# Keys and the second layer's first product as seven products of quarters, in a two-layer graph kernel on one core

## The chip, the cores and the metric

The kernel runs on one core of a Trainium2 chip. The metric is the device time of one launch in microseconds, and less is better. The engines are named as the profile names them: PE (TensorE, matrix products), DVE (VectorE), ACT (ScalarE), POOL (GpSimd), and SP (SyncE, whose queue issues most of the loads). Each engine takes its instructions in the order in which the kernel issued them, and waits at each for what it needs from the others.

## The reference, cut to what matters

There are 16 graphs of 1024 nodes and 256 channels, which share one adjacency matrix. Layer 0 is attention whose queries come from a product with a weighted adjacency, and layer 1 is a graph convolution with two dense products and batch norms over all graphs.

```
# layer 0, per graph; h = relu(layernorm(x))
Wg  = adj * A_s(mean of h)                       # 1024 x 1024
q   = relu((h^T @ Wg) * para)                    # "queries"
k,v = split(h @ kv_w)                            # "keys", "values"
x   = x + softmax(q k^T) v                       # 4 heads
# layer 1; h = relu(layernorm(x))
agg = (D^-1/2 (adj + I) D^-1/2) @ h              # "aggregate"
y1  = agg @ W1^T + b1                            # 256 -> 512, "hidden"
out = batchnorm(relu(batchnorm(y1)) @ W2^T + b2) # needs all graphs
x   = x + out
```

## The kernel before, in words

All numbers are float32. The first part of the kernel, `layers`, handles the 16 graphs one after the other; the second part, `second`, runs the last product and the batch norms once all graphs have gone through. The change is in the first part, whose order is written out by hand.

**Attention sets the beat.** `attention` (L1092) goes through 16 steps for each graph. A step issues two tiles of scores (`scores`, L923: PE products `sc`, then the exponential on ACT into `p`), then the two additions of `p` to the running sums (`Unit.add`, L956, on DVE: `acc`), then the product of the previous step's `p` with the values (`Unit.values`, L967, PE: `o`). There are two score tiles in PSUM and four `p` tiles in SBUF.

**The rest is background.** While graph b is in attention, `background(b)` (L835) does the other work in small pieces: graph b+1's keys, values and queries, and graph b-1's second norm, aggregate and hidden product. Each piece yields a cost (1.71 for two products), and `attention` takes pieces at the end of each step until the sum of their costs reaches what is due (`total`, L1108). A side generator in `weave` (L148) is advanced once with each piece of the main one. An action given to `soon` (L128) is issued after the next piece. So the order of the instructions on every engine follows from these costs.

**Pieces that the change touches.**
- `product` (L167) is one product of 128 x 128 by 128 x 512, in two halves of 64 rows. `bank` (L164) gives it one of the three PSUM tiles of `ps_mm` (L118), in turn; a tile comes round again at the third next call, and its first product then waits until the reader of the old contents is done.
- `keys_values` (L649): four keys banks of two products each (L657), copied by ACT (L660), then four values banks (L669), copied by ACT (L677).
- `weigh` (L454) makes the weighted adjacency: 17 slots, in turn two ACT operations `Abs` (L485), one `Tanh` (L493), and with every second slot one DVE operation (L472).
- `queries` (L514) makes its product as seven products of quarters, each four inner products long; `take` (L548) and `finish` (L534) are DVE work. Its four `para` loads (L528) go round two buffers, so each waits on SP until the user of the buffer before is done.
- `aggregate` (L682) is also seven products of quarters. Its 14 loads `aht` (L693) go on SP's queue, five ahead, into the buffers of the weights `w`. Four DVE operations scale its result by the roots of the degrees (`scale`, L705).
- `hidden` (L757): eight banks of two products, each read by ACT with the bias (L773), written out by a DMA on POOL's queue (L774), with statistics on DVE (L777).
- `normed` (L790) writes x away (`keep`), normalises, and loads the graph after the next two (L796). `load_x` (L173) goes round three buffers.
- `graph` (L244), once, in graph 0's background: POOL combines quarters of the adjacency and writes them out as `aht_d`. `degrees` (L225), once, computes the degrees. `load_later` (L290), once, loads W1 and broadcasts the roots.
- `differences` (L428) sends the column sums of a graph out and broadcasts them back into `cbc`, which the `Abs` operations read.
- `prepare` (L812) issues a graph's transposition by way of DRAM (`squares`, `gathered`) and its first weight slots along with the hidden product.

Seven products of quarters means the Winograd form of Strassen's method: for a product of two 2 x 2 arrangements of blocks, seven block products in place of eight, with sums of blocks before and after.

Of the kernel before, what the change touches and what calls it, by code (L numbers as in the profile page):

```python
# [17 lines left out]
P = 128  # L18
# [5 lines left out]
def gnn_two_layers_kernel(  # L24
# [34 lines left out]
    vec = const.tile([P, 18], F32, name="vec")  # L59
    nc.sync.dma_start(out=vec, in_=vecs)  # L60
    b1, g1, be1 = (vec[:, i * HC : (i + 1) * HC] for i in range(3))
    b2, g2, be2 = (vec[:, 3 * HC + i * CC : 3 * HC + (i + 1) * CC] for i in range(3))
# [34 lines left out]
    def layers(shifted):  # L97
# [13 lines left out]
        py = st.enter_context(tc.tile_pool(name=f"py_{kind}", bufs=4))  # L111
# [7 lines left out]

        xs, hs, hts, ats, qs, ks, vs = {}, {}, {}, {}, {}, {}, {}  # L120
        invs = {}
        csums, cbcs, weighted, weighers = {}, {}, {}, {}
# [50 lines left out]
        def load_x(b):  # L173
            xs[b] = p3.tile([P, NT, C], F32, tag="x", name=f"x_{b}")
            parts = 4 if b == 0 else 2
            for part in range(parts):
                t = slice(part * NT // parts, (part + 1) * NT // parts)
                nc.sync.dma_start(
                    out=xs[b][:, t], in_=x[b].rearrange("(t p) c -> p t c", p=P)[:, t]
                )  # L180
# [44 lines left out]
        def degrees():  # L225
# [16 lines left out]
            rsqrt(dinv, deg, 1.0, tmp_deg)  # L242

        def graph():  # L244
# [21 lines left out]
            for u in range(2 * HT):  # L266
# [3 lines left out]
                for n in range(2):  # L270
                    if part == t * P // HB:
                        blk = a[:, n, n, t * P % HB : t * P % HB + P]
                        nc.gpsimd.tensor_add(blk, blk, ident)
                two = py.tile([P, 2, HB], F32, tag="y", name=f"two_{u}")
# [14 lines left out]

        def load_later():  # L290
            later["w1"] = big.tile([P, CC, H1], F32, tag="w1", name="w1")
            nc.sync.dma_start(out=later["w1"], in_=w1_t.rearrange("(k p) j -> p k j", p=P))
            later["dbc"] = const.tile([P, N], F32, tag="dbc", name=f"dbc_{kind}")
            nc.sync.dma_start(out=dinv_d.rearrange("(t p) -> p t", p=P), in_=dinv)
            nc.sync.dma_start(
                out=later["dbc"], in_=dinv_d.rearrange("(o n) -> o n", o=1).to_broadcast([P, N])
            )

        class Norm:
# [3 lines left out]
            def __init__(self, b, first):  # L303
                tag = "a" if first else "b"
                self.src = xs[b]
# [343 lines left out]
        def keys_values(b):  # L649
            ht = hts[b]  # L650
            ks[b] = [p4.tile([P, N], F32, tag="k", name=f"k_{b}_{k}") for k in range(CC)]
            for g in range(NH):
                for j in range(CC):
# [7 lines left out]
                    yield 1.71  # L661

            vs[b] = [p4.tile([P, NT, P], F32, tag="v", name=f"v_{b}_{k}") for k in range(CC)]
# [18 lines left out]
        def aggregate(b):  # L682
# [3 lines left out]
            order = (0, 2, 5, 1, 4, 6, 3)  # L686
# [18 lines left out]
            def scale(c, g):  # L705
                nc.vector.tensor_mul(c, c, later["dbc"][:, g * FB : (g + 1) * FB])

# [4 lines left out]
            def second(m):  # L712
                add(c11, m, c12)
                sub(a12, a12, a11)
                soon(lambda: scale(c11, 0))

            def fifth(m):
                add(c22, m, c21)
                add(c12, m, c12)
                soon(lambda: scale(c22, 1))  # L720

            def sixth(m):
                add(c21, m, c21)
                soon(lambda: scale(c21, 0))

            def seventh(m):
                add(c12, m, c12)
                scale(c12, 1)

            for i, (left, after) in enumerate(  # L730
# [5 lines left out]
                    (None, fifth),  # L736
                    (a22, sixth),
                    (a12, seventh),
# [4 lines left out]
                for th in range(NP // 2):  # L743
# [9 lines left out]
                    elif i == 0:  # L753
                        combine("b", b, nc.vector)
                    yield 1.71

        def hidden(b):  # L757

# [31 lines left out]
        def normed(b):  # L790
# [4 lines left out]
            if b + 3 < B:  # L795
                load_x(b + 3)  # L796
# [15 lines left out]
        def prepare(b, products):  # L812
# [4 lines left out]
            if b == 2:  # L817
                for k in range(CC):
                    yield from weave(islice(products, 3), (0, islice(w, AHEAD // 2)))
                    yield TOP  # L820
                    transposed(b, (k,))
                    yield 1.0
                yield from products
                return
            squares(b)
            yield from weave(islice(products, 3), (0, islice(w, AHEAD // 2)))
            gathered(b, 0)
            yield from weave(islice(products, 1), (0, islice(w, 1)))
            gathered(b, 1)
            yield from weave(islice(products, 2), (0, islice(w, AHEAD // 2 - 1)))  # L830
# [4 lines left out]
        def background(b):  # L835

            if b == 0:
# [6 lines left out]
                yield from weave(  # L844
# [719 lines left out]
```

## Time and profile before

| What | us |
|---|---|
| Median of the 3 runs (2488.99 to 2489.55) | 2489.24 |
| The profiled execution | 2488.76 |
| Its span, first to last instruction | 2487.0 |
| PE clock granted, mean | 0.993 |
| Start of graph 1, 2, 3 in attention | 166.9, 304.1, 440.1 |
| ACT L660, copies of keys, 64, each | 0.579 |
| ACT L773, hidden product with bias, 128, each | 0.683 |
| DVE L706, scaling of the aggregate, 64, each | 0.674 |
| DVE L965, addition to the sums, 384, each | 1.227 |
| DVE L734, addition from PSUM, 16, each | 0.685 |

The profile is of one execution. A group of its instructions has a line of the kernel, an engine, the output and the inputs by their names in the program, the count, the busy time and the mean of one, and then the time for which the engine had been idle, with what ended it. In a timeline the columns are start and duration in us, engine, line, operation and operands, and how many instructions were merged into the row.

### The profile page before, as it was taken

How to read it: one execution, taken by the hardware profiler on the slowest of the kernel's cores; microseconds unless marked ns; L12 is line 12 of the kernel's file. 1: busy time of each engine (PE TensorE's matmuls, PEld its weight loads, DVE VectorE, ACT ScalarE, POOL GpSimd, SP SyncE). 2: the span in 40 equal slices, each digit the busy share in tenths (PEclk: the TensorE clock that was granted, in tenths of full speed). 3: DMA queues.
4: the chain of work that ended last, by engine and by line, in shares of the span. 5: the costliest groups of instructions: out<-in, count | busy, mean ns of one | idle time of the engine just before them, and what ended most of it. 6: DMA issues, size and time to landing. Idle time of an engine off the chain costs nothing. (4 is left out here: it accounts for less than half of the span.)

```text
span 2487.0 us, 35569 instructions
## 1 busy us (share of the span) xinstructions
PE 2435.7 (98%) x13403; PEld 841.2 (34%) x13403; DVE 1882.0 (76%) x2920; ACT 1401.7 (56%) x1927; POOL 429.2 (17%) x527
## 2 busy tenths in 40 slices
PE   9999999999999999999999999999999999999995
PEld 4333333333333333333333333333333332334444
DVE  5668787877778787878787787868787877767775
ACT  7775564647473746656474747465564634345544
POOL 1640101010101001011101010110101001036652
PEclk9999999999999999999999999999999999999997
DMA  4754535354545545362645445543536344355559
GB/s 150 238 173 172 170 114 199 101 199 129 197 145 178 164 159 169 116 206 84 215 126 182 145 174 169 178 153 132 191 94 210 116 140 162 132 214 220 189 199 374
DMA packets 187909, 421.42 MB, mean 169 GB/s; under 512 B 21832, under 2 KB 81744, under 8 KB 181968
## 3 DMA queue, kind: packets, MB, share of 16 engines
q1 hardware_dynamic: 158560, 311.56, 37.9%
q0 software_dynamic: 29168, 107.50, 11.6%
q8 instruction: 108, 1.77, 0.3%
q14 instruction: 73, 0.60, 0.1%
HBM read 315.63 MB, written 103.35 MB: 168 GB/s over the span
## 5 line engine op out<-in xcount | busy, mean ns | idle before, releaser
L941 ACT ACTIVATE p<-sc 128x1024 f32<-128x1024 f32 x512 | 494.9, 1019 | 617.6 <-PE sc L933 617.2
L965 DVE TENSOR_TENSOR acc<-acc,p 128x1024 f32<-128x1024 f32 x384 | 471.3, 1227 | 165.1 <-ACT p L941 143.8
L933 PE MATMUL sc<-q,k 64*64 64x512 f32 x4096 | 498.8, 602 | 6.2 <-ACT p L941 6.2
L976 PE MATMUL o<-p,v 128*64 128x512 f32 x2048 | 494.5, 604 | 0.3 <-DVE os L990 0.3
L171 PE MATMUL pg<-w,h_a 128*64 128x512 f32 x1600 | 359.8, 592 | 0.8 <-DVE w L472 0.8
L171 PE MATMUL pa<-aht,h_b 128*64 128x512 f32 x1536 | 346.0, 592 | 1.1 <-ACT h_b L342 1.0
L485 ACT ACTIVATE w<-cbc,csum 128x512 f32<-128x512 f32 x256 | 285.8, 1168 | 0.0
L933 PEld LDWEIGHTS sc<-q,k 64*64 64x64 f32 x4096 | 131.0, 132 | 347.9 <-issue 286.5
L472 DVE SCALAR_TENSOR_TENSOR w<-w,adj 128x1024 f32<-128x1024 f32 x128 | 156.9, 1225 | 95.0 <-ACT w L493 91.1
L171 PE MATMUL py<-at,w 128*64 128x512 f32 x1024 | 228.4, 592 | 0.2 <-ACT y L773 0.2
L976 PEld LDWEIGHTS o<-p,v 128*64 128x64 f32 x2048 | 124.4, 136 | 298.3 <-issue 260.3
L994 POOL DMA_DIRECT2D out_d<-os x58 | 34.2, 590 | 1070.8 <-DVE os L990 1037.5
L171 PEld LDWEIGHTS pg<-w,h_a 128*64 128x64 f32 x1600 | 114.8, 137 | 229.2 <-issue 218.8
L171 PEld LDWEIGHTS pa<-aht,h_b 128*64 128x64 f32 x1536 | 109.9, 137 | 215.3 <-issue 202.0
L773 ACT ACTIVATE y<-py,vec 128x512 f32<-128x512 f32 x128 | 87.4, 683 | 115.4 <-PE py L171 91.8
L493 ACT ACTIVATE w<-w 128x1024 f32<-128x1024 f32 x128 | 135.1, 1055 | 1.7
L774 POOL DMA_DIRECT2D y_d<-y x128 | 69.7, 545 | 371.8 <-ACT y L773 362.6
L548 DVE TENSOR_TENSOR w<-w,w 128x1024 f32<-128x1024 f32 x112 | 132.7, 1214 | 1.5
L171 PEld LDWEIGHTS py<-at,w 128*64 128x64 f32 x1024 | 74.0, 137 | 145.5 <-issue 131.5
L171 PE MATMUL pv<-kvw_f,ht 128*64 128x256 f32 x1024 | 116.1, 379 | 0.0
L171 PE MATMUL pk<-ht,kvw_f 128*64 128x512 f32 x512 | 115.2, 592 | 0.2 <-ACT ht L404 0.2
L342 ACT ACTIVATE h_b<-x,lnsm_b 128x256 f32<-128x256 f32 x128 | 69.9, 599 | 65.9 <-DVE lnsm_b L331 65.9
(169 smaller groups left out, 2665.4 us busy)
## 6 DMA issues: line engine op xcount, KB each, us to landing
aht<-aht_d SPq DMA_DIRECT2D x224, 512.0 KB, 6.4
adj<-in_adj_dram SPq DMA_DIRECT2D x128, 512.0 KB, 4.8
y_d<-y POOLq DMA_DIRECT2D x128, 256.0 KB, 3.0
yin_f<-y_d SPq DMA_DIRECT2D x32, 1024.0 KB, 6.4
para<-in_para_dram SPq DMA_DIRECT2D x64, 256.0 KB, 3.6
x_d<-x POOLq DMA_DIRECT2D x16, 1024.0 KB, 5.2
xo_f<-x_d SPq DMA_DIRECT2D x32, 512.0 KB, 8.2
out_dram<-xo_f POOLq DMA_DIRECT2D x32, 512.0 KB, 10.8
```

What stands on the lines that cost most here:

```text
L171: nc.tensor.matmul(dst[r], left[:, r], right, start=start, stop=stop)
L342: nc.scalar.activation(self.h[:, t, :], self.src[:, t, :], AF.Relu, bias=self.sm[:, 1, t : t + 1], scale=self.sm[:, 0, t : t + 1], accum_o ...
L472: nc.vector.scalar_tensor_tensor(w, w, 1.0, a, op0=ALU.add, op1=ALU.mult)
L485: nc.scalar.activation(w[:, t, :].rearrange("p (t q) -> p t q", q=P), cbc[:, q * NT // NH : (q + 1) * NT // NH], AF.Abs, bias=csum[:, th * ...
L493: nc.scalar.activation(made[i], made[i], AF.Tanh, scale=-0.5 / C)
L548: nc.vector.tensor_sub(block(i)[part], block(x)[part], block(y)[part])
L773: nc.scalar.activation(y, made, AF.Identity, bias=b1[:, j : j + 1])
L774: nc.gpsimd.dma_start(out=y1_d[i][:, j, :], in_=y)
L933: nc.tensor.matmul(sc[part, e, :], ks[b][k][r, m * P + c * HW : m * P + (c + 1) * HW], qs[b][k][r, f * FB : (f + 1) * FB], start=True, sto ...
L941: nc.scalar.activation(pr, sc, AF.Exp)
L965: nc.vector.tensor_add(self.acc, self.acc, pr)
L976: nc.tensor.matmul(self.o[r, :], vs[b][k][:, m, r], pr[:, e, :], start=(m == 0), stop=(m == NT - 1),)
```

## The change

- **Keys** of graphs 3 to 15 (`keys_of`, behind `values_of`): seven products of quarters, one product to a bank, on blocks of the transposed h. ACT copies two of the seven banks, DVE adds the other five into the result. POOL makes two sums of blocks before (`key_steps`), two in between, and two sums of results.
- **Hidden product** of graphs 0 to 13: twice seven products, one product to a bank, in an order written out. ACT reads four of the 14 banks, DVE ten. POOL adds four times. The blocks' sums are made at the end of the aggregate (`steps_of`, three subtractions on DVE) and at the start of the hidden product (one). Graphs 14 and 15 keep the old form (`plain_hidden`).
- **Weights**: eleven slots of `weigh` go one to a piece with the values and keys, the others one to a piece with the queries (before: four, then two to a piece). In `background(b)`, from b = 2 on, all values and keys stand ahead of the queries; before, the values stood behind them.
- **x** is loaded twice, into one buffer for each use: `xn` for the first norm, at the start of `background`, and `xr` for the residual, at the end of `normed`. The first output of a graph is added one step later than before (`wait` 6 for 5).
- **The scaling by the roots of the degrees** moves from DVE in each aggregate to POOL in `graph`, once; the roots are broadcast at the end of `degrees`, ahead of `differences(2)`, and `graph` runs from the end of graph 0's background into graph 1's.
- The sums of blocks of the weights are made once, on POOL (`combined` in `load_later`). The tiles `y` are six for four. The last two products of the aggregate change places. The costs that pace the background follow.

```diff
         def keys_values(b):
+            if b > 2:
+                yield from values_of(b)
+                yield from keys_of(b)
+                return
...
+        def keys_of(b):
...
+            t1, t2 = steps.pop(b)
+            nc.gpsimd.tensor_sub(b12, b22, b12)
+            add = nc.vector.tensor_add
+
+            def second(m):
+                add(c11, m, c12)
+                nc.gpsimd.tensor_sub(b21, b21, t2)
+
+            def fifth(m):
+                add(c21, m, c12)
+                nc.gpsimd.tensor_add(c12, c12, c22)
+                nc.gpsimd.tensor_add(c22, c22, c21)
+
+            for i, (left, right, after) in enumerate(
+                (
+                    (a11, b11, lambda m: nc.scalar.copy(c12, m)),
+                    (a12, b21, second),
+                    (s1, t1, lambda m: nc.scalar.copy(c22, m)),
+                    (s2, t2, lambda m: add(c12, m, c12)),
+                    (s3, b12, fifth),
+                    (s4, b22, lambda m: add(c12, m, c12)),
+                    (a22, b21, lambda m: add(c21, m, c21)),
+                )
+            ):
+                made = bank(f"pk_{b}_{i}")
+                product(made, left, right, True, True)
+                after(made)
+                yield 0.86
...
         def hidden(b):
+
+            if b >= B - 2:
+                yield from plain_hidden(b)
+                return
...
+            def m1(c):
+                part = one("1", a11, c, b11)
+                nc.scalar.activation(
+                    new("11", c), part, AF.Identity, bias=b1[:, c : c + 1]
+                )
+
+            def m2(c):
+                y = made["11"]
+                add(y, one("2", a12, c, b21), y)
+                put(y, 0, c)
+
+            def m3(c):
+                y = made["12"]
+                add(y, one("3", s4, c, b22), y)
+                put(y, 1, c)
+
+            def m4(c):
+                y = made["21"]
+                add(y, one("4", a22, c, t4), made["sum"])
+                put(y, 0, 2 + c)
+
+            def m5(c):
+                nc.scalar.copy(new("22", c), one("5", s1, c, t1))
+                if c == 1:
+                    both(c)
+
+            def both(c):
+                nc.gpsimd.tensor_add(new("12", c), made["21"], made["22"])
+
+            def m6(c):
+                y = new("21", c)
+                add(y, one("6", s2, c, t2), made["11"])
+                if c == 0:
+                    both(c)
+
+            def m7(c):
+                part, y = one("7", s3, c, t3), made["22"]
+                nc.vector.scalar_tensor_tensor(
+                    new("sum", c), part, b1_step[:, c : c + 1], made["21"], op0=ALU.add, op1=ALU.add
+                )
+                nc.gpsimd.tensor_add(y, y, made["sum"])
+                put(y, 1, 2 + c)
+
+            for c, order in ((0, (m1, m5, m6, m2, m3, m7, m4)), (1, (m1, m6, m2, m5, m7, m3, m4))):
+                for each in order:
+                    each(c)
+                    yield 0.86
...
             yield from Norm(b, False).all()
-            if b + 3 < B:
-                load_x(b + 3)
+            load_x(b + 1)
...
             rsqrt(dinv, deg, 1.0, tmp_deg)
+            dbc = big.tile([P, 4, H1 // 2], F32, tag="w1s", name="dbc")
+            dbc = later["dbc"] = dbc.rearrange("p a b -> p (a b)")
+            nc.sync.dma_start(out=dinv_d.rearrange("(t p) -> p t", p=P), in_=dinv)
+            nc.sync.dma_start(
+                out=dbc, in_=dinv_d.rearrange("(o n) -> o n", o=1).to_broadcast([P, N])
+            )
...
+                dinvs = later["dbc"].rearrange("p (m c) -> p m c", m=NH)[:, :, cols]
+                for n in range(2):
+                    nc.gpsimd.tensor_mul(a[:, n], a[:, n], dinvs)
+                yield 0.0
...
             gather = aggregate(b - 1)
             if b + 1 < B:
                 w, products, norm = weighers[b + 1], keys_values(b + 1), normed(b - 1)
-                yield from weave(islice(products, 4), (0, islice(w, 4)))
+                build = later.pop("graph", iter(()))
                 if b == 1:
...
                     load_later()
-                yield from weave(queries(b + 1), (0, double(w)), (9, islice(norm, 5)))
+                else:
+                    yield from weave(products, (0, islice(w, 11)))
+                    yield from weave(queries(b + 1), (0, w), (6, norm))
                 yield next(gather)
                 yield from weave(products, (0, norm))
```

## The prediction

> **What bounds the kernel now.** I read the page first, for the busy shares, then who made PE wait, then one graph in the middle (847.9 to 983.9 us) by stretches, then the timelines of PE, ACT, DVE and SP through that graph.
>
> ```profile
> PE 2435.7 (98%) x13403; PEld 841.2 (34%) x13403; DVE 1882.0 (76%) x2920; ACT 1401.7 (56%) x1927; POOL 429.2 (17%) x527
> ```
>
> Busy share alone does not settle it, so the next view is PE's waits (total us, times, longest):
>
> ```profile
> PE sc L933 <- ACT p L941: 6.2, 5, 2.5
> ...
> PE pa L171 <- ACT h_b L342: 1.0, 1, 1.0
> ...
> PE py L171 <- ACT y L773: 0.2, 1, 0.2
> ```
>
> The whole list, 14 rows, comes to 21 us. One graph of the steady middle, in four stretches summed:
>
> ```profile
> sum 136.00, PE 136.00 PEld 43.97 DVE 107.24 ACT 78.40 POOL 14.16; mean PE 34.00 PEld 10.99 DVE 26.81 ACT 19.60 POOL 3.54
> ```
>
> PE is busy for 136.00 of 136.00 us. Every graph from 2 to 13 starts 135.96 us after the one before. So each microsecond of PE taken away is a gain, and each one in which PE must wait is a loss. Nothing else counts here.
>
> The price of a product comes from PE's timeline (start, us; the first row of each step is sc):
>
> ```profile
> 883.65 1.95 PE L933 MATMUL sc<-q,k 64*64 64x512 f32 x16
> 885.52 1.94 PE L976 MATMUL o<-p,v 128*64 128x512 f32 x8
> 887.29 3.60 PE L171 MATMUL pg<-w,h_a 128*64 128x512 f32 x16
> 890.83 1.95 PE L933 MATMUL sc<-q,k 64*64 64x512 f32 x16
> 892.70 1.94 PE L976 MATMUL o<-p,v 128*64 128x512 f32 x8
> 894.47 5.32 PE L171 MATMUL pg<-w,h_a 128*64 128x512 f32 x24
> 899.72 1.95 PE L933 MATMUL sc<-q,k 64*64 64x512 f32 x16
> ```
>
> A step with two parts of background lasts 7.18 us (883.65 to 890.83), one with three 8.89: a part of two products costs 1.71, one product 0.857, scores and values 3.7.
>
> **The gain.** Keys of graphs 3 to 15 need 7 products for 8: 13 fewer. The second layer's first product of graphs 0 to 13 needs 14 for 16: 28 fewer. 41 x 0.857 = 35.1 us. The profiled execution took 2488.76 (span 2487.0; median of the runs 2489.24), so with nothing else changed 2453.6.
>
> **What evacuates the products.** Before, a bank of these two stages held two products (1.71 us) and ACT emptied it. Now each product has its own bank (still three in ps_mm), so a bank must be emptied within two further products, 1.71 us, and mostly by DVE. Per graph DVE gets 10 adds for the second layer, 4 subtractions for its steps and 5 adds for the keys, and loses 4 scalings: 15 x 0.69 (rows of 128x512) = 10.4 us, 107.2 to 117.6 of 133.4 us. That fits on average. But in each step the two acc additions stand ahead of the background's work in DVE's order, and they wait for the step's exponentials on ACT. That order sets three stalls. Below, t is counted from the start of step 0 of a graph, with distances between starts in the timelines.
>
> **Keys (step 2).** The changed order puts the four value products and all seven key products into steps 0 to 2, with one weight slot on each. ACT has no idle time from the first value product (t = 5.6) on. Up to the exponentials of step 2 it has four pairs of value copies (0.52 each), four pairs of L485 (2.25), three L493 (0.95), two key copies (0.48) and the exponentials of step 1 (1.84): 2.1 + 9.0 + 2.8 + 1.0 + 1.8 = 16.7. So those of step 2 start at t = 22.4, 5.4 into the step. The old kernel shows the same lateness (step 2 began at 865.74, its exponentials at 871.54):
>
> ```profile
> 866.27 1.06 ACT L493 ACTIVATE w<-w 128x1024 f32<-128x1024 f32 x1
> ...
> 868.18 2.37 ACT L485 ACTIVATE w<-cbc,csum 128x512 f32<-128x512 f32 x2
> 870.58 1.06 ACT L493 ACTIVATE w<-w 128x1024 f32<-128x1024 f32 x1
> 871.54 1.92 ACT L941 ACTIVATE p<-sc 128x1024 f32<-128x1024 f32 x2
> ```
>
> ```profile
> 872.58 2.56 DVE L965 TENSOR_TENSOR acc<-acc,p 128x1024 f32<-128x1024 f32 x2 [2.28 <-ACT p L941]
> ```
>
> The acc pair then takes 23.4 to 25.8, and the add that empties the fourth key product ends at 26.4. The seventh takes the same bank and is due at 16.9 + 3.7 + 3 x 0.857 = 23.2. PE stands for **3.2 us**. The old kernel bore this because ACT emptied its key banks in ACT's own order and a query product fills a bank for 3.4 us. Lower end: exponentials 1 us earlier, 2.2. Upper: POOL's two additions on c12 and c22 collide with DVE's weight product (below), 4.0. 13 graphs: 42 us (29 to 52).
>
> **Second layer's first product (steps 13 to 15).** t' from step 13. DVE: acc to 4.4, one subtraction, two squares 2.3 (to 7.35), two adds (8.6), transpose and sum (9.95); step 14: acc after the exponentials to 12.6, m3's add 13.2, a weight product 14.35, statistics 14.95, m7's add 15.65. The fifth product after m3 (m6 of the second half) needs m7's bank, and would start at 14.3: it waits **1.4 us**. The walk of step 15 finds no further wait. Lower 0.5, upper 3 if DVE enters step 13 late. 13 graphs: 19 us (6 to 39).
>
> **Loads (step 8).** SP takes its DMAs in order. Before, the order was para, os, five aht, then x:
>
> ```profile
> 868.87 37.97 SPq L528 DMA_DIRECT2D para<-in_para_dram  x3
> 906.93 1.80 SPq L1000 DMA_DIRECT2D os<-out_d  x4
> 908.85 2.49 SPq L693 DMA_DIRECT2D aht<-aht_d  x5
> 916.77 0.94 SPq L178 DMA_DIRECT2D x<-in_x_dram  x2
> ```
>
> The last para waited for DVE's product with an earlier para until 906.84; aht went at 908.85, 6.9 us ahead of pa (915.73), and lands in 4.3 to 10.2. In the changed order the queries start three key products later, pa follows them at once (the four value products that lay between are gone to the front), and the reload of x, which waits for the last h_b, stands ahead of aht. Walking DVE on from the key stall (steps 5 and 6 hold 13.2 and 8.6 us of rows against 8.9 and 8.9 of PE), the para product ends 1.3 us into step 8. Then para, two x (0.94 us of issue) and aht: aht leaves about 3 us into step 8 behind 1.25 MB. At 0.41 MB/us (DMA packets of the trace between 912 and 916, summed), with 2 us to the first bytes, it lands at 8 us; pa is due at 3.8. Stall 4.2 by the walk, 0.1 if DVE were not late, 5.5 if it is later still. I take **3.5**, nearer the walk since DVE was 5 us late at this place already (897.58 for exponentials ready by 893). 13 graphs: 46 us (1 to 72). The reload itself (1 MB a graph more) is due only two steps later and is covered.
>
> The rest of the change costs nothing that I can find: the tail after graph 15 is the same code, the output of each graph's first unit is added two steps later and nothing waits for it but the next norm, and the DVE scalings that go were off PE's path.
>
> **Graphs 0 and 1, once.** The roots of the degrees are now written to DRAM and broadcast back ahead of the column sums of graph 2, on the same queue. What SP waited for then (120 to 260 us):
>
> ```profile
> SPq L295 <- DMA dinv_d<-deg: 10.4, 1, 10.4
> ...
> SPq L450 <- DMA csum_d<-csum: 3.9, 1, 3.9
> ```
>
> The degrees are ready at 139.7, the root at 142; 10.4 us for the write, then 3.9 for the sums' write and 5.8 for their broadcast (its landing before): 163. ACT's first weight of graph 2 now stands at step 12 (about 146 us into the span; 153 before) and blocks the exponentials behind it. Two score buffers cover one step: some 13 us later. POOL then scales and combines the adjacency with 16 more operations of 128x512; with 12 us a piece for eight pieces it ends near 250, about when graph 0's aht is wanted: 5 more. 18 us (5 to 30).
>
> **POOL beside DVE.** An operation of 128x512 on POOL does not occur before; 128x256 takes 0.73 and 128x1024 2.36, so 1.2 to 1.5, ten a graph. What one does to DVE is seen once at the end (start, us):
>
> ```profile
> 2227.67 2.67 DVE L1382 TENSOR_TENSOR y_f<-y_f,y_f 128x512 f32<-128x512 f32 x1
> ```
>
> ```profile
> 2227.45 2.35 POOL L1327 TENSOR_TENSOR t_f<-yin_f,yin_f 128x1024 f32<-128x1024 f32 x1
> ```
>
> An addition of 0.68 with both inputs in SBUF took 2.67, until POOL was through. On the 13 acc additions that met a POOL operation the mean is 1.48 for 1.22, so ten cost 2.6 us a graph, which is inside the upper ends. The Trainium skill (SBUF — State Buffer, Who interferes with whom) has it as an exclusive lock held for the whole instruction, the other fully blocked; if all ten met the start of one, DVE would lose some 12 us a graph and have 129 of 133 us filled. That would speak against the change even on average.
>
> **Sum.** 2488.8 - 35.1 + 42 + 19 + 46 + 18 = 2578.7. I forecast **2578**.
>
> **Rivals.**
> Loads hidden: DVE catches up while PE stands at the keys, para is free in step 7 and aht is in time. Without that term 2533. For it: the x load of before rode behind aht with no wait. Against: order on SP.
> Evacuation in time, faster: 2454, or 2472 with the loss in graphs 0 and 1. For it: PE waits for nothing now, DVE has 24% left. It decides only if the exponentials of step 2 start 3.2 us earlier (t = 19.2), so that the fourth key bank is empty in time, and the aht loads leave in step 7. Against it: the ACT sum above has no idle time in it to give back.
> The port of DVE and POOL makes DVE the bound in steps 0 to 3 and 13 to 15, so that the 2.6 us a graph reach PE: 13 x 2.6 = 34 more, 2612.
> That the products are not fewer is excluded: the built order of PE has three fewer in each graph from 2 to 13.
>
> **Numbers.** All three stalls, 2550 to 2600: 0.50. Loads hidden, 2495 to 2550: 0.25. Port, 2600 to 2650: 0.12. In time, 2454 to 2484: 0.10. Between, within 0.2% of before (5 us, about what a measurement of this kernel can tell from no change): 0.03. So slower 0.87, same 0.03, faster 0.10. The lower ends of the terms sum to 2495, the upper ones to 2647; the range 2495 to 2625 leaves out the faster case (0.10), no change (0.03) and the upper half of the port's (0.06).
>
> **What would show it.** In the new profile: PE waiting for DVE k at the keys' product, 13 times near 3 us; for DVE y at py, near 1.4; for DMA aht at pa, 13 times some 3 to 4; a gap of ACT near 146 to 163 and PE sc waiting for ACT p there. Graphs of about 141 us for 135.96. Wrong: graphs of 133.4 and no such rows, or the waits at other places.

## The result, and the profile of the changed kernel

The changed kernel takes 2701.18 us (median of 4 runs, 2699.18 to 2702.23) for 2489.22 before: a ratio of 1.085, 95% interval 1.0832 to 1.0869. Slower was right; the size was not: 2578 was forecast and 2625 was the upper end. The profiled execution took 2702.05, with a span of 2700.2.

First come the page's busy shares, then PE's main waits, with the wait of ACT that explains the last of them (total us, times, longest):

```profile
PE 2479.2 (92%) x13239; PEld 845.2 (31%) x13239; DVE 2068.1 (77%) x3117; ACT 1357.8 (50%) x1845; POOL 687.0 (25%) x686
```

```profile
PE pa L174 <- DMA aht<-aht_d: 83.3, 13, 6.7
...
PE pk L174 <- DVE k L721: 43.3, 12, 4.0
...
PE py L174 <- DVE y_sum L930: 17.0, 13, 1.3
PE sc L1125 <- ACT p L1133: 16.5, 2, 16.2
ACT w L513 <- DMA cbc<-csum_d: 16.2, 1, 16.2
```

PE's waits are at the four places that the prediction named, and add up to 160 us. But the kernel is 213 us longer although 35 us of products are gone, so 248 have to be found. PE's two long waits in the steady graph from 938.2, and SP's queue ahead of the second:

```profile
965.17 1.92 PE L174 MATMUL pk<-ht,kvw_f 128*64 128x512 f32 x4 [3.58 <-DVE k L721]
...
1020.88 8.25 PE L174 MATMUL pa<-aht,h_b 128*64 128x512 f32 x24 [6.20 <-DMA aht<-aht_d]
```

```profile
1013.15 0.35 SPq L556 DMA_DIRECT2D para<-in_para_dram  x1
1013.60 0.94 SPq L183 DMA_DIRECT2D xr<-in_x_dram  x2
1014.64 14.84 SPq L785 DMA_DIRECT2D aht<-aht_d  x11
```

The six products at pa take 8.25 us, where six of the same shape take 5.32 in the kernel before. The windows of the same graph show why (columns: window, its length, busy us and number of instructions on PE, PEld, DVE, ACT and POOL, clock granted to PE as a share of the full one, DMA share, GB/s):

```profile
962.00:965.17 3.17, 0.00 (x1) 0.03 (x1) 2.96 (x4) 3.17 (x4) 0.00 (x0) 1.00 0.45 143
965.17:968.00 2.83, 2.83 (x8) 1.15 (x10) 1.78 (x2) 1.81 (x2) 2.04 (x1) 0.52 0.00 0
...
1014.70:1020.90 6.20, 0.02 (x2) 0.05 (x2) 3.95 (x6) 1.51 (x2) 0.65 (x1) 0.92 1.02 350
1020.90:1024.00 3.10, 3.10 (x8) 1.06 (x10) 0.00 (x0) 0.00 (x0) 0.00 (x0) 0.50 1.03 404
1024.00:1027.00 3.00, 3.00 (x10) 0.94 (x8) 0.00 (x0) 0.00 (x0) 0.00 (x0) 0.55 1.03 418
1027.00:1030.00 3.00, 3.00 (x22) 0.86 (x22) 2.00 (x3) 1.12 (x2) 0.00 (x0) 1.00 1.03 415
```

After each of these waits PE works at half the full clock: some 3.4 us behind the wait at the keys, some 6 behind the one at pa, where 8 to 10 matmuls pass in 3 us and then 22. The mean granted clock, 0.962 for 0.993 before, says that something is there, but not where; a step whose wait and products are known, and whose length they do not explain, shows the place. By starts of steps, the graph from 938.2 takes 150.0 us. 133.4 of it are products and scores, 5.5 go at the keys (step 2), 9.3 at pa (step 8), 1.9 at the hidden product.

### The profile page after: what moved, and what is told of

Same layout as the page of the kernel before. It is cut to its first block, busy times and chain, and to the rows that moved or that the text cites. A ratio compares the mean times of both kernels' runs of the same rounds, so it can differ in the third digit from the quotient of the medians.

```text
span 2700.2 us, 35921 instructions
## 1 busy us (share of the span) xinstructions
PE 2479.2 (92%) x13239; PEld 845.2 (31%) x13239; DVE 2068.1 (77%) x3117; ACT 1357.8 (50%) x1845; POOL 687.0 (25%) x686
## 5 line engine op out<-in xcount | busy, mean ns | idle before, releaser
L1157 DVE TENSOR_TENSOR acc<-acc,p 128x1024 f32<-128x1024 f32 x384 | 489.4, 1275 | 102.9 <-ACT p L1133 79.7
L174 PE MATMUL pa<-aht,h_b 128*64 128x512 f32 x1536 | 378.8, 642 | 84.4 <-DMA aht<-aht_d 83.3
L174 PE MATMUL pg<-w,h_a 128*64 128x512 f32 x1600 | 372.5, 612 | 4.6 <-DVE h_a L586 4.6
L513 ACT ACTIVATE w<-cbc,csum 128x512 f32<-128x512 f32 x256 | 287.9, 1180 | 16.2 <-DMA cbc<-csum_d 16.2
L174 PEld LDWEIGHTS pa<-aht,h_b 128*64 128x64 f32 x1536 | 119.7, 148 | 331.0 <-issue 279.8
L500 DVE SCALAR_TENSOR_TENSOR w<-w,adj 128x1024 f32<-128x1024 f32 x128 | 185.4, 1449 | 43.2 <-ACT w L521 42.3
L174 PE MATMUL py<-at,w1s 128*64 128x512 f32 x448 | 107.3, 598 | 17.0 <-DVE y_sum L930 17.0
L1154 DVE TENSOR_TENSOR acc<-p,p 128x1024 f32<-128x1024 f32 x64 | 78.6, 1228 | 52.5 <-ACT p L1133 52.4
L174 PE MATMUL py<-at,w 128*64 128x512 f32 x464 | 115.3, 595 | 2.1 <-DVE y L906 0.9
L174 PE MATMUL pk<-ht,kvw_f 128*64 128x512 f32 x252 | 69.7, 673 | 43.7 <-DVE k L721 43.3
L1497 ACT ACTIVATE yin_f<-yin_f,sm_f 128x512 f32<-128x512 f32 x128 | 93.5, 803 | 14.3 <-DMA yin_f<-y_d 14.0
```

Of the source, the lines that this page charges most:

```text
L174: nc.tensor.matmul(dst[r], left[:, r], right, start=start, stop=stop)
L500: nc.vector.scalar_tensor_tensor(w, w, 1.0, a, op0=ALU.add, op1=ALU.mult)
L513: nc.scalar.activation(w[:, t, :].rearrange("p (t q) -> p t q", q=P), cbc[:, q * NT // NH : (q + 1) * NT // NH], AF.Abs, bias=csum[:, th * ...
L1154: nc.vector.tensor_add(self.acc, self.held, pr)
L1157: nc.vector.tensor_add(self.acc, self.acc, pr)
L1497: nc.scalar.activation(y, y, AF.Relu, bias=sh[:, j : j + 1], scale=scale[:, j : j + 1])
```

## The experiments

The theory is that each wait is set by the order of instructions on one queue (SP's at pa, ACT's at the keys, DVE's at the hidden product), and that a long wait costs a stretch at half clock besides. The rivals are named run by run. Times are medians; the kernel before took 2489.0 to 2489.4 beside each of them. A steady graph is one of graphs 3 to 13.

### x behind the aht loads

```diff
             yield from Norm(b, False).all()
-            load_x(b + 1)
...
                 yield next(gather)
                 yield from weave(products, (0, norm))
+                load_x(b)
...
```

> The changed kernel with one move: the second load of x is issued behind the first five aht loads instead of ahead of them. In the steady graph from 938.2 of the changed kernel's trace the last para leaves SP at 1013.15, x at 1013.60, the first aht at 1014.64, and PE stands 6.20 us for it until 1020.88, then runs at half clock (0.50 to 0.55 granted) until 1027, which costs some 3 more: step 8 lasts 18.3 for 9.0. Theory (SP's order sets the wait, and half a clock follows a long wait): aht leaves at 1013.6 and no longer shares the way with 1 MB of x, lands in the 4.3 us of the fastest load of the kernel before, 1017.9; stall 3.2 instead of 6.2, half clock shorter or gone. 13 graphs by 3 to 6 us: 2623 to 2662. Rival (the five aht loads, 2.5 MB, set the landing by their own travel): step 8 stays near 18, 2690 to 2701.

It took 2645.93 us (ratio 1.063, 1.0612 to 1.0648), as the theory said. PE's 13 waits at pa fell from 83.3 to 41.8 us. In graphs 2 to 13 they are now 3.1 to 3.9 long, and the clock drops in some of these graphs (step 8 mostly lasts 13.9 to 14.2) and not in others (12.3 to 12.6).

### Two aht loads ahead of the last para

```diff
+            load(1)
+            yield 0.0
             load(4)
             yield 0.0
...
-                    yield from weave(queries(b + 1), (0, w), (6, norm))
+                    yield from weave(queries(b + 1), (0, w), (6, norm), (11, islice(gather, 1)))
```

> As the run with x behind, and the first two aht loads are also issued ahead of the last para load, right behind the sixth product of the queries, whose weights' buffers they take; the other three follow where the five stood. Theory: the first aht no longer waits on SP for DVE's product with para, leaves some 4 us earlier than in the changed kernel (about 1009.5 to 1010 in the graph from 938.2), lands by 1014.5, when pa is due at 1014.7; no wait and so no half clock: step 8 about 9.0 for 18.3, 13 x 9.3 = 121 us less, 2580 (2570 to 2600). Rival (travel, or the buffers come free too late): a wait of 2 to 3 us is left, step 8 at 11 to 13, 2610 to 2640. Rival 2 (the later three loads now stand behind the last para): the wait moves to the third piece of pa.

It took 2582.30 us (1.0372, 1.0355 to 1.0389), 118.9 less than the changed kernel, which is the theory to 2 us. The products at pa follow attention's (`o`) at once and at full speed:

```profile
975.33 1.92 PE L1174 MATMUL o<-p,v 128*64 128x512 f32 x8
977.08 5.32 PE L174 MATMUL pa<-aht,h_b 128*64 128x512 f32 x24
```

Step 8 lasts 9.0 to 9.6 us for 18.3, with the same loads: its loss came from their order on SP. How long a load travels counted within it. In the run before this one, PE had aht 4.2 us after it left, behind para alone, and in the changed kernel 6.2, behind para and x; that is 2 of the 3 us by which the wait fell there.

### The weights spread

```diff
-                    yield from weave(products, (0, islice(w, 11)))
+                    yield from weave(products, (0, islice(w, 4)), (7, islice(w, 4)))
```

> The changed kernel with the weight slots of ACT placed otherwise: four with the value products, none with the first three key products, four with the last four, the last three with the queries (changed kernel: eleven, one to each piece of values and keys). Theory (the exponentials of step 2 are late since ACT has seven weight slots ahead of them, and DVE's additions wait for them with the key addition behind): three slots fewer ahead, about 4.5 us (two Abs pairs or Tanh of 2.4 and 1.06); exponentials of step 2 start when the scores are there, the stall of 3.58 at the key product and the 1.9 of half clock after it go: step 2 lasts 8.9 for 14.39, 13 x 5.5 = 71 us less, 2630 (2625 to 2645). Rival (POOL's four additions hold DVE, which lost 2 us in steps 1 and 2 by them): the stall stays at 2 or more, 2665 to 2701. Rival 2: the weights are late for the queries, PE waits at pg in steps 3 and 4 by 1 to 3 us.

It took 2635.63 us (1.0588, 1.057 to 1.0606), 65.6 less than the changed kernel; step 2 lasts 9.07 for 14.39. In the changed kernel ACT reached the exponentials of step 2 (from 955.20) only at 960.83, in this run (step 2 from 931.11) at 932.26. First the changed kernel's ACT, then this run's:

```profile
957.13 1.06 ACT L521 ACTIVATE w<-w 128x1024 f32<-128x1024 f32 x1
958.09 0.57 ACT L720 COPY k<-pk 128x512 f32<-128x512 f32 x1
958.56 2.36 ACT L513 ACTIVATE w<-cbc,csum 128x512 f32<-128x512 f32 x2
960.83 1.92 ACT L1133 ACTIVATE p<-sc 128x1024 f32<-128x1024 f32 x2
```

```profile
932.26 1.94 ACT L1133 ACTIVATE p<-sc 128x1024 f32<-128x1024 f32 x2 [0.45 <-PE sc L1125]
```

POOL's additions slowed DVE in step 1 in both kernels (the acc pair took 3.44 and 3.45 us for 2.56), and only one of them lost time. So the rival, that POOL holds DVE, falls here. Nor are the weights late: PE waits 6.0 us for DVE's products with them in all, for 5.8 in the changed kernel.

### The roots behind the column sums, and no scalings on POOL

```diff
             rsqrt(dinv, deg, 1.0, tmp_deg)
+
+        def roots():
...
                 differences(2)
+                roots()
                 w, build = weighers[2], graph()
```

> The changed kernel with the write and the broadcast of the roots of the degrees issued behind the column sums of graph 2 instead of ahead of them. Theory (SP stands 11.6 us for the roots' write, so the column sums leave at 151 and their broadcast frees ACT at 159.6, 16.2 us late): the wait of ACT and PE's 16.2 us near 148 to 164 go, graph 0 lasts 110 for 124.6: 2701 - 14 = 2687; POOL's graph build then starts no earlier. Rival (the column sums themselves are late, or ACT's weights wait for something else): no change, 2698 to 2702.

It took 2698.23 us (1.0835, 1.0817 to 1.0854): 3 less, where 14 were expected. The wait did go (graph 0 takes 105.8 us for 124.6), but graph 1 takes 170.5 for 156.6. The second run asks why, and leaves the scaling out altogether:

```diff
-                for n in range(2):
-                    nc.gpsimd.tensor_mul(a[:, n], a[:, n], dinvs)
```

> As the run with the roots behind, with POOL's 16 scalings of the adjacency left out, so the aggregate is of the unscaled adjacency (20 us of POOL fewer, nothing else). Theory (POOL's operations hold DVE, whose additions take 2.2 to 2.9 for 1.22 while POOL builds, and graph 1 lasts 170.5 since PE waits for DVE until POOL is through): POOL is through 20 us earlier, graph 1 lasts 145 to 155, 2675 to 2685. Rival (DVE has too much of its own to do in graph 1, or the adjacency loads pace the build): graph 1 stays within 5 us of 170, 2693 to 2698.

It took 2677.05 us (two executions), and graph 1 150.9. Its aggregate is that of the unscaled adjacency, so the run is for the timing alone. The windows of graph 1 in the kernel before, with the roots behind, and without scalings:

```profile
166.90:304.10 137.20, 137.18 (x792) 44.72 (x792) 107.18 (x164) 80.06 (x110) 13.13 (x20) 1.00 0.48 158
```

```profile
159.70:330.20 170.50, 143.39 (x788) 45.60 (x788) 138.46 (x173) 80.54 (x109) 106.61 (x117) 0.93 0.57 191
```

```profile
160.20:311.10 150.90, 140.31 (x784) 44.76 (x784) 124.19 (x173) 80.43 (x109) 84.04 (x99) 0.97 0.64 213
```

The same 173 operations take DVE 138.5 us with the roots behind and 124.2 without scalings (107.2 for 164 in the kernel before). With 22.6 us less on POOL, PE is through graph 1 19.6 earlier. Its waits there are for DVE, 27 us with the roots behind and 10.5 without scalings. So the wait in graph 0 was cover. POOL starts to scale at about 155 us in both kernels; in the changed kernel it was busy for 28.6 us of graph 0, which the wait made longer, and with the roots behind for 12.8. With that wait gone, PE stands in graph 1 for a DVE that POOL slows.

### The wait at pa filled with work

```diff
                     load(n + 5)
+                    if n == 0 and b < B - 2:
+                        for _ in range(7):
+                            product(made, left[:, 0, :], kvw[:, 0, :], True, True)
```

> The changed kernel with seven products into the first pa bank ahead of the aggregate's first product, whose results are overwritten by it (they need nothing but h_b and the weights of keys and values, and last 6.0 us at full clock): work added, in the place of PE's wait of 6.2 us for the first aht. Theory (after a wait the granted clock is 0.50 for one or two stretches of 3.413 us by the clock records, which at pa costs some 3 us a graph): PE is not idle, the clock stays at 1.0, the six products after it take 5.3 instead of 8.25, step 8 lasts 15.3 for 18.3: 13 x 3.0 = 39 less, 2662 (2655 to 2668), although PE does 6 us more a graph. Rival (the products after the wait are slow because the loads beside them are in the way, at 400 GB/s): pa stays at 8 us, 2701 or up to 10 more.

It took 2679.77 us (1.077, 1.0754 to 1.0787): 21 less, with 6 us more work in each of 14 graphs. The six products after it run at full clock, with the same loads beside them (417 GB/s meanwhile, for 404 to 418 in the changed kernel):

```profile
1011.97 6.18 PE L174 MATMUL pa<-kvw_f,h_b 128*64 128x512 f32 x28
1018.94 5.37 PE L174 MATMUL pa<-aht,h_b 128*64 128x512 f32 x24 [0.80 <-DMA aht<-aht_d]
```

They take 5.37 us for 8.25, so the loads were not in the way. Step 8 of graphs 2 to 13 takes 15.4 to 16.2, for 15.3 expected; the total misses by 18. About half of that is graph 1, which was counted as a gain of 3: PE had no wait at pa there, and pays the filling in full (6.0). At the keys the drop now lasts longer in some graphs (step 2 15.3 for 14.4).

### Three moves together, then the hidden product's slot

The first run joins the moves of the x, aht and weights runs. The second adds to it:

```diff
-            yield from weave(islice(products, 5), (0, islice(w, AHEAD // 2)))
+            yield from weave(islice(products, 5), (0, islice(w, AHEAD // 2 - 1)))
             gathered(b, 0)
-            yield from weave(islice(products, 3), (0, islice(w, 1)))
+            yield from weave(islice(products, 3), (0, islice(w, 2)))
...
-                soon(lambda: nc.vector.bn_stats(stats1[:, j, i, :], y))
+                soon(lambda: soon(lambda: nc.vector.bn_stats(stats1[:, j, i, :], y)))
```

> Three moves at once: x behind the aht loads, two aht loads ahead of the last para, weights spread. By themselves the last two runs took 118.9 us (2701.2 to 2582.3) and 65.6 us (to 2635.6) away. Theory (two waits with causes of their own): the gains add, 2701.2 - 184.5 = 2516.7, 2510 to 2522; steady graphs 135.3 (133.4 and 1.9 at the hidden product). Rival (both waits gave DVE time to catch up, so the one that goes makes another late): 2530 to 2560, with PE waiting at pa or pg again.

> As the run with three moves, and in the hidden product the third early weight slot (DVE's product with the adjacency) goes behind the seventh product of the first half, and the statistics of y are issued one piece later. Theory (PE's 1.31 at py each graph is the wait for the bank that DVE empties with y_sum, and ahead of it stand 1.22 of weights and 0.69 of statistics that nobody waits for): the wait goes or falls under 0.2, 13 x 1.3 to 1.9 = 17 to 25 us less than the run with three moves, so about 2495. Rival (DVE is short of time there, whatever the order): the wait moves to another bank, less than 5 us.

The first took 2526.18 us (1.0144, 1.0127 to 1.0161): the gains add but for 9.5. Step 8 lasts 9.8 to 10.7, since the third aht load still leaves behind para. The second took 2519.83 (1.0122, 1.0106 to 1.0139): 6 less, for the 17 to 25 expected. PE's waits at py, the hidden product, fell from 17.0 to 12.3 us and stand behind another bank, y of L903. The rival of that run was nearer: there the bank's addition stands right behind the acc pair, 2.56 us.

### The scaling back on DVE, and the plain hidden product

```diff
-                for n in range(2):
-                    nc.gpsimd.tensor_mul(a[:, n], a[:, n], dinvs)
...
+            def scale(c, g):
+                nc.vector.tensor_mul(c, c, later["dbc"][:, g * FB : (g + 1) * FB])
...
-                yield from weave(plain_queries(1), (0, w), (4, norm), (7, degrees()))
+                yield from weave(
+                    plain_queries(1), (0, w), (4, norm), (5, graph()), (7, degrees())
+                )
```

> As the run with the hidden slot, and the scaling by the roots of the degrees goes back to DVE in each aggregate (four products of 128x512), the graph's build back to graph 0 without scalings, and the roots' broadcast back to the loads of graph 1. To make room the tiles y are five for six, in another order. Theory (POOL's build with its scalings, beside DVE in graph 1, and the roots ahead of the column sums cost graphs 0 and 1 some 31 us: 124.6 and 156.6 in the changed kernel for 111.9 and 137.2 before): these go, 31 less than the run before it, 2465, which is 1% under the kernel before; the four scalings (2.7 us of DVE a graph) lie in steps 9 to 13, where DVE waits for PE. Rival: the scalings stand ahead of what PE waits for at py, 0.7 to 1.5 a graph in 13 graphs, 2474 to 2485. Rival 2: graphs 0 and 1 stay long for another reason, 2490 to 2500.

It took 2500.75 us (1.0042, 1.0027 to 1.0056), 19 less than the run before it for the 31 expected. Graph 0 takes 105.8, but graph 1 147.1: the adjacency loads stood behind the roots' write on SP, DVE stood 6.7 us for them, and PE 7.4 for DVE (0.2 in the next run, where these loads go first). Steady graphs take 136.4 to 137.0 (136.63 on average, for 136.13 in the run before it), so the scalings, with five tiles `y` for six, cost half a microsecond a graph.

The next run takes the old form of the hidden product in all graphs:

```diff
-            if b >= B - 2:
+            if b >= 0:
                 yield from plain_hidden(b)
                 return
...
-                    load_later()
                     yield from weave(queries(2), (0, double(w)), (9, islice(norm, 5)))
+                    load_later()
```

> As the run with the scaling back on DVE, with the second layer's first product in its old form in all graphs (eight banks of two products, read by ACT), and the loads of W1, roots and sums of weights in graph 1 behind the queries, since the adjacency load behind them was 7 us late there. In the run with the scaling back a steady graph took 136.5, of which steps 14 and 15 18.2 for the 16.1 that their products and scores make; graph 1 took 147 for 137. Theory (what the 14 products save, 1.71 a graph, is about what their banks' waits on DVE cost, 2.1): graphs 136.2, graph 1 10 us shorter: 2487 (2482 to 2492). Rival (the waits were those of weights or scaling and stay): graphs of 138, 2510 to 2520.

It took 2499.55 us (1.0041, 1.0025 to 1.0056): the total misses by 12.5, since in graph 1 the roots' write now made aht late (a wait of 11.9 us). The question was the steady graph: it takes 136.25 on average, for 136.63 with fourteen products. So the hidden part of the change is worth nothing here: with it steps 14 and 15 take 18.2 us for the 16.1 of their products and scores, and these 2.1 are more than the 1.71 of the two products that it saves.

### The keys alone, in the kernel before

Three runs put the keys part alone into the kernel before, with x loaded twice as in the change. In the first the keys stand first, the values behind the queries as before, and the sums of blocks in tiles of their own. The second makes these sums at the end of the graph before (and issues aht ahead of the last norm), the third one piece earlier still:

```diff
+            sub(t1, b12, b11)
+            sub(t2, b22, t1)
+            sub(t3, b22, b12)
+            sub(t4, b21, t2)
...
-                yield from weave(islice(products, 4), (0, islice(w, 4)))
+                n = 7 if b > 1 else 4
+                yield from weave(islice(products, n), (n - 4, islice(w, 4)))
...
```

> The kernel before with the keys part alone: keys of graphs 3 to 15 as seven products, one to a bank, but first in the background as the keys were before, with the values still behind the queries; the sums of blocks go into tiles of their own (room from the two x buffers of the changed kernel), and the four weight slots come with the last four key products. Theory (the seven products cost PE time only where DVE's or ACT's order makes their banks late; in step 0 ACT and DVE had some 3 us idle each before the key copies, and the values between the queries and the aggregate still cover the aht loads): no wait at pk or pa, 13 x 0.857 = 11.1 us less, 2478 (2474 to 2484). Rival (banks of one product need an answer within 1.71 us and DVE's additions to the sums stand ahead wherever they are put): a wait of 0.9 or more at pk, 2489 or longer. Rival 2 (the extra MB of x a graph makes pa wait): PE pa <- DMA rows.

It took 2533.23 us (1.0178, 1.0164 to 1.0192), 55 more than forecast. PE has no wait for DVE at the keys, but waits 27 us there for POOL's sums, and 14.1 at pa, once, in the last graph, behind x on SP. Behind the waits at the keys the clock went to a half in four graphs of thirteen, not at each, as the expectation of the next run has it.

```diff
             yield from products
+            step_keys(b)
...
-                yield from weave(endings.pop(), (2, normed(b - 1)))
                 yield next(gather)
+                yield from weave(endings.pop(), (2, normed(b - 1)))
```

> As the run with the keys alone, with two moves: POOL makes the four sums of blocks at the end of the graph before (there they stood behind POOL's wait for the output's copy, so that PE waited 1.69, 0.27 and 0.16 us for them at each step 0 and the clock went to a half), and in the last graph the aht loads are issued ahead of the norm, as in the changed kernel (there x went first, and PE waited 14.1 us). Theory (those two orders were all that was lost): step 0 lasts 8.9 for 11.7, graphs of 135.1 for 137.9, no wait in graph 15: 2489.0 - 11.1 = 2478 (2474 to 2482), under both kernels. Rival (the key banks of step 0 then wait for DVE's additions to the sums, 3 us after the values): a wait of 0.5 to 2 at pk <- DVE k, 2485 to 2505.

It took 2498.58 us (1.0038, 1.0024 to 1.0052). PE has the rival's wait, 1.49 us at the second product's bank. DVE and POOL at the start of one such step 0 (from 1671.1):

```profile
1672.99 1.62 DVE L1153 TENSOR_TENSOR os<-os,inv 128x512 f32<-128x512 f32 x1
1674.64 1.64 DVE L1161 TENSOR_TENSOR xr<-os,xr 128x512 f32<-128x512 f32 x1
1676.21 2.29 DVE L1041 TENSOR_TENSOR acc<-p,p 128x1024 f32<-128x1024 f32 x1
1678.42 0.70 DVE L1069 STREAM_TRANSPOSE os<-o 128x512 f32<-128x512 f32 x1
1679.05 0.65 DVE L723 TENSOR_TENSOR k<-pk,k 128x512 f32<-128x512 f32 x1
```

```profile
1672.76 1.28 POOL L697 TENSOR_TENSOR kt<-ht 128x512 f32<-128x512 f32 x1
1674.12 1.61 POOL L698 TENSOR_TENSOR kt<-ht,kt 128x512 f32<-128x512 f32 x1
1675.70 1.72 POOL L699 TENSOR_TENSOR kt<-ht,ht 128x512 f32<-128x512 f32 x1
1677.38 2.25 POOL L700 TENSOR_TENSOR kt<-ht,kt 128x512 f32<-128x512 f32 x1
```

The first three rows of DVE read two tiles in SBUF. Each begins while one of POOL's is under way and ends 0.55 to 1.08 us after that one; POOL's next, begun meanwhile, ends 1.1 us after DVE's. So they go in turn. The addition from PSUM (0.65, last row) is not held.

```diff
-            yield from weave(islice(products, 2), (0, islice(w, AHEAD // 2 - 1)))
-            yield from products
-            step_keys(b)
+            yield from weave(islice(products, 1), (0, islice(w, 1)))
+            step_keys(b)
+            yield from weave(islice(products, 1), (0, islice(w, 1)))
+            yield from products
...
-                    (a12, b21, lambda m: add(c11, m, c12)),
                     (s1, t1, lambda m: nc.scalar.copy(c22, m)),
+                    (a12, b21, lambda m: add(c11, m, c12)),
```

> As the run with the sums of blocks at the end of the graph before, with those four operations of POOL one piece earlier still (in a stretch in which POOL waited 4.1 us for ACT, and DVE 1.3 us), and with the third key product ahead of the second, so that the first two banks are ACT's. In the run before it DVE's rows at the start of step 0 lasted 1.62, 1.64 and 2.29 us for 0.67, 0.69 and 1.22 while POOL made its sums, 3.0 us in all, and PE waited 1.49 us for the bank of the second product. Theory (POOL's operations beside DVE's are what is left of the keys' cost, 1.5 us a graph): no wait at pk, step 0 lasts 9.0 for 10.6, graphs of 135.1 for 136.81: 2498.6 - 13 x 1.6 = 2477 (2474 to 2482), under both kernels. Rival (DVE's own order, the additions to the sums ahead of the evacuation, sets the wait): the wait falls by half at most by the exchange of the products, 2486 to 2494.

It took 2476.33 us (ratio 0.9951, 0.9937 to 0.9964), under both kernels and within 1 us of the forecast of 2477. A steady graph, and DVE's rows at its start:

```profile
844.00:979.10 135.10, 135.10 (x782) 43.76 (x780) 111.80 (x172) 77.54 (x106) 23.75 (x29) 1.00 0.49 167
```

```profile
846.97 0.67 DVE L1154 TENSOR_TENSOR os<-os,inv 128x512 f32<-128x512 f32 x1
847.68 0.69 DVE L1162 TENSOR_TENSOR xr<-os,xr 128x512 f32<-128x512 f32 x1
848.29 1.22 DVE L1042 TENSOR_TENSOR acc<-p,p 128x1024 f32<-128x1024 f32 x1
849.42 0.71 DVE L1070 STREAM_TRANSPOSE os<-o 128x512 f32<-128x512 f32 x1
850.51 0.69 DVE L724 TENSOR_TENSOR k<-pk,k 128x512 f32<-128x512 f32 x1 [0.38 <-PE pk L172]
```

PE is busy for 135.10 of 135.10 us: 135.96 less one product. DVE now waits for the product (0.38 at L724). The two moves of this run were not made apart; that DVE is ahead of PE at this addition says that the exchange of the products was not needed, but this is argued, not shown.

## Why the prediction was wrong

The waits stood, in place and in kind. What failed is their price. The prediction says of PE that "each one in which PE must wait is a loss. Nothing else counts here", and so counts each wait at its own length; the runs show a stretch at half clock behind each long one, which no term held. Besides, the loads' term was too small. Term by term, by the profiled execution (from 2488.8 to 2578.7 by the sum; measured 2702.05):

- **Gain, 35.1.** It stands: a graph without waits is 133.4 (135.96 less three products), and the waits and slow stretches found add up to the 150.0 measured.
- **Keys, 42.** The wait was put at 3.2 us and is 3.58, in the forecast's place and by its chain (exponentials at t = 22.4, measured 22.6). The price failed: slow products cost 1.9 us more behind it, which makes 5.5 a graph, 71 in 13. The weights run shows it (65.6 gained).
- **Second layer, 19.** The wait is 1.31 for 1.4; with smaller waits around it the cost is 1.9 a graph, 25 in all.
- **Loads, 46.** This term was furthest off: 3.5 us were taken where the walk gave 4.2, and the wait is 6.2. The walk had the last para free 1.3 us into step 8 and aht leave at about 3; para left 2.4 in and aht 3.9 in (1014.64), and PE had it 6.2 us later, behind para and x, for the 5 of the walk. (Its 0.41 MB/us is 0.40 by the window 912 to 916, which changes little.) Then the half clock cost 3.1 us more: 9.3 a graph, 121 in 13. The aht run shows the sum of both (118.9 gained), and the run with the wait filled shows the half clock apart from the loads.
- **Graphs 0 and 1, 18.** They take 32 more. The wait for the column sums is 16.2 us for the 13 forecast, and POOL's build beside DVE, put at 5, goes with most of the rest. The roots run and the one without scalings show that the two cover each other: POOL alone would hold graph 1 back.
- **Rivals.** "Loads hidden" fell at once. The port as the bound of the steady graph fell too: taking ACT's weights away removed the keys' wait with POOL's operations still there. In graph 1 it did bind.

Of the 123 us that the sum lacks, 60 are half clock in the steady graphs (4.6 a graph: 6.8 us at pa, of which 1 lies in the wait, and 3.4 at the keys, half of each), 35 the longer wait at pa (2.7 a graph), 14 graphs 0 and 1, and 14 the rest, in the keys' and the hidden waits. The range was too narrow because each term was bounded by its wait alone: even the upper ends of all terms together give 2647.

## What to carry to other kernels

A wait on PE costs its length and then, if the clock drops, the slow stretch behind it. Here waits of about 3 us or more mostly cost 1.5 to 3.1 us beyond their length, so price a wait with that on top. A saving on the engine that bounds is worth what it is only if the answers that it needs (here one evacuation for each product, for each second one before) come from an engine with nothing ahead of them in its order; walk each queue up to that instruction, SP and POOL too. Try the parts of such a change one by one: of this one, the keys alone pay (0.5%), once POOL's sums stand where they hold up nothing that PE needs, and the hidden product does not.

## What the runs showed of the hardware

- **Half clock in fixed stretches.** The clock records of these traces hold 1.0 or 0.5, for multiples of 3.413 us. In the changed kernel the waits of 6.2 to 6.7 us at pa came with 6.8 us at half, in all thirteen graphs (in the steady ones the stretch begins about 1 us before the wait ends), and those of 3.57 to 3.60 at the keys with 3.4, in the steady graphs. Length alone does not decide. Of the twelve waits of 3.10 to 3.87 us at pa in graphs 2 to 13 of the run with x behind, eight had it, one of 3.10 among them, and one of 3.38 had not. The keys' wait of graph 14 had it in the changed kernel (2.37 us), but not in the runs with x behind, aht ahead and the wait filled (2.35 to 2.38). Two of 2.9 in graph 1 of the changed kernel had it; of its thirteen of 1.31 one had it, right behind another of 0.6. The Trainium skill (TensorE: Matmul & The Clock Gate, Part 1: The HAM clock gate) names windows of about 3.4 us that run freely, and a half clock after an idle one. The stretches agree in length, and windows that run freely would explain why equal waits differ. Its rule to leave no gap over some 3.4 us (HAM oscillation — how this bites in real kernels) is too mild here, since 2.9 was enough twice and 2.4 once.
- **Who is held beside POOL.** In the run with the sums at the end of the graph, DVE's rows with two inputs in SBUF took 1.61 us for 0.68 (os), 1.65 for 0.69 (xr) and 2.29 for 1.23 (acc) on average of the 13 beside POOL's sums. Transposes (0.70), statistics (0.68) and additions from PSUM (0.65) kept their time. POOL's operations of 128x512 took 1.28 where DVE did not hold them and up to 2.26. The Trainium skill (SBUF — State Buffer, Who interferes with whom) says just this of two SBUF inputs against a POOL operation that reads SBUF.
